# Transposes of the attention heads in two row tiles, the distance term summed on TensorE

## The chip, the cores and the metric

The kernel runs on one core of a Trainium2 chip. The metric is the device time of one execution in microseconds, the median of several runs. The core has five engines that run beside one another and wait for each other through semaphores: TensorE (PE, with its weight loads PEld), VectorE (DVE), ScalarE (ACT), GpSimd (POOL) and SyncE (SP), which issues DMAs. Each engine works through its instructions in the order in which the program gives them. SBUF is the working memory; TensorE writes into the eight banks of PSUM.

## The reference, cut to what matters

The program is a chain of four parts on a sequence of 2 x 1024 rows of 128 numbers: a Mamba block, a mixture of experts, six encoder layers (`L1_attn`), and a feed-forward part with 4-bit quantisation. The change is in the encoder. One of its layers is:

```python
rel = jnp.exp(-jnp.abs(pos[:, None] - pos[None, :]).astype(x.dtype) / DECAY)
...
scores = jnp.einsum('bhld,bmhd->bhlm', q, k) * inv_sqrt_d
w_avg = jax.nn.softmax(scores, axis=-1).mean(axis=1)
new_w = jax.nn.softmax(CSCALE * w_avg + rel[None], axis=-1)
sa = jnp.einsum('blm,bme->ble', new_w, h)
h1 = _ln(h + sa, l1w, l1b)
h2 = _ln(h1, l2w, l2b)
ff = jax.nn.relu(h2 @ w1.T + b1_) @ w2.T + b2_
return (_ln(h2 + ff, l3w, l3b), None)
```

There are H = 16 heads of 8 numbers, L = 1024 positions, 2 sequences and 6 layers, CSCALE = 1 and DECAY = 16. So each query has sixteen softmax rows of 1024, their mean, plus a term `rel` that depends on the distance alone, a second softmax, and a product with `h`.

## The kernel before

The encoder is the class `Encoder`. One attention is one layer of one sequence: 8 tiles of 128 queries (`m`), each with 16 heads (`hh`), 128 steps in all; 12 attentions make 1536 steps. `run` (L1067) writes the order of all engines out by hand, one step `s` after the other. A tile of 128 queries has its scores in 16 steps; the later stages of the same tile follow some steps behind. In each step:

- `scores` (L947): two matmuls of bf16 parts (72 x 128 weights, 72 x 512 moving, L963) put one head's scores of 128 queries into `sc`, a PSUM tile of two banks, of which there are three. VectorE takes the negated maximum `nm` of each row (L966).
- `exponentials` (L969): ScalarE writes `e = exp(sc + nm)` to SBUF and the row sums `z` with it (L972). The pool of `e` has 13 buffers.
- `scaled` (L981): every fourth step (GT = 4), VectorE takes the reciprocals of four heads' sums (L986), and GpSimd multiplies the four `e` by them (L989).
- `added` (L991), LAG = 10 steps behind: TensorE transposes the scaled `e` into `acc`, where the heads add up. A transpose is a matmul with a block of `e` (128 queries x 128 keys) as weights and the identity as the moving operand, and it accumulates in PSUM (L1008). `acc` is two tiles of one bank, each for 512 of the 1024 keys. In each of the four steps of a group of four heads, eight transposes are made: two heads in one half of the keys. Within a bank, the blocks of keys stand in reverse order.
- `shifted` (L1018), for each half of the keys: when its last head is in, VectorE forms `acc / 16 + rel` into the SBUF tile `mean` (L1022). `rel` is one array of 1920 columns, of which each tile takes a window.
- `second` (L1032): ScalarE takes the exponential of `mean` into `prT` (L1035). The two halves come two steps apart.
- `mixed` (L1043), four steps after the second of them: TensorE multiplies the transposed weights by `h`, with a column of ones for the sum (16 instructions at L1048, into `sa`, which is again one of the three score buffers). `residual` (L1057), one step later: VectorE divides and adds `h`.

Everything else of a layer (`between`, L885: norms, feed-forward with L904 and L918, transposes at L752; `project`, L810, for the next layer's queries and keys at L829, with their DMAs) is written as generators. `advance_one` (L1105) issues one piece of them in each step in which `mixed` doesn't stand, and two in each fourth.

TensorE's order in a step is therefore: scores, transposes, then a piece or the final product. The other engines see scores first, then the reductions, the scaling, the exponentials, then the second exponential.

Of the kernel before, what the change touches and what calls it, by code (L numbers as in the profile page):

```python
# [11 lines left out]
F32 = mybir.dt.float32  # L12
BF16 = mybir.dt.bfloat16
AF = mybir.ActivationFunctionType
ALU = mybir.AluOpType
# [3 lines left out]
P = 128  # L19
EPS = 1e-5  # L20
B, L, D = 2, 1024, 128
NT = B * L // P
TB = L // P
# [5 lines left out]
NL, NH, DH, FF = 6, 16, 8, 512  # L29
# [606 lines left out]
class Encoder:  # L636
# [10 lines left out]
    ROWS = 9 * DH  # L647
    GH = 4
    GT = 4
    LAG = 10  # L650
    TH = TB // 2
    HL = L // 2

    def __init__(self, c, ctx, x, w, t):
        self.c, self.nc, self.tc = c, c.nc, c.tc
        self.x, self.w, self.t = x, w, t
        nc, tc = self.nc, self.tc
        pool = lambda name, bufs, **kw: ctx.enter_context(tc.tile_pool(name=name, bufs=bufs, **kw))
# [12 lines left out]
        self.scale = float(DH) ** -0.5  # L671
        wp = self.wp

        nrel = 2 * L - P
        self.rel = wp.tile([P, nrel], F32, name="rel")
        nc.gpsimd.iota(
            self.rel,
            pattern=[[-1, nrel]],
            base=L - P,
            channel_multiplier=1,  # L680
            allow_small_or_imprecise_dtypes=True,
        )
        nc.scalar.activation(self.rel, self.rel, AF.Abs, bias=c.zero)
        nc.scalar.activation(self.rel, self.rel, AF.Exp, bias=c.zero, scale=-1.0 / DECAY)

        self.cols = {}
        for k in ("b1", "bq", "bk"):
            n = t[k].shape[0]
            src = t[k]
            if k != "b1":  # L690
                src = wp.tile([n, DH, NH], F32, name=f"e_{k}o")
                nc.gpsimd.tensor_copy(src, t[k].rearrange("l (h d) -> l d h", d=DH))
                src = src.rearrange("l d h -> l (d h)")
            ps = self.psum(f"ps_e_{k}")
            nc.tensor.transpose(ps[:, :n], src, c.ident[:n, :n])
            self.cols[k] = wp.tile([P, n], F32, name=f"e_{k}")
            nc.scalar.mul(self.cols[k], ps[:, :n], self.scale if k == "bq" else 1.0)
        self.eps = wp.tile([P, 1], F32, name="eps")
        nc.gpsimd.memset(self.eps, EPS)
        self.weights = {}  # L700
        self.h = [None] * B
        self.hn = [None] * B
        self.r = [None] * B
        self.qk = [None] * B
# [283 lines left out]
            e = a["e", s + i]  # L988
            nc.gpsimd.tensor_scalar(e, e, rz[:, i : i + 1], 1.0, ALU.mult, ALU.mult)  # L989

    def added(self, a, s, i):  # L991

        m, hh = divmod(s, NH)
        if hh == 0 and i == 0:
            a["acc", m] = [
                self.psa.tile([P, 4, P], F32, tag=f"acc{k}", name=f"acc_{a['who']}_{m}_{k}")
                for k in range(2)
            ]  # L1000
        half, two = divmod(i, 2)
        for j in (2 * two, 2 * two + 1):
            e = a["e", s + j]
            if half:
                del a["e", s + j]
            for n in range(4):
                at = (4 * half + n) * P
                self.nc.tensor.matmul(  # L1008
                    a["acc", m][half][:, 3 - n, :],
                    e[:, at : at + P],  # L1010
                    self.c.ident,
                    is_transpose=True,
                    start=hh + j == 0 and n == 0,
                    stop=hh + j == NH - 1,
                    skip_group_check=True,
                )

    def shifted(self, a, m, half):  # L1018

        t = self.loop.tile([P, self.HL], F32, tag="mean", name=f"mean_{a['who']}_{m}_{half}")  # L1020
        at = L - P - (4 * half + 3 - m) * P
        self.nc.vector.scalar_tensor_tensor(  # L1022
            t,
            a["acc", m][half].rearrange("p n q -> p (n q)"),
            1.0 / NH,
            self.rel[:, at : at + self.HL],
            ALU.mult,
            ALU.add,
        )
        a["mean", m, half] = t  # L1030

    def second(self, a, m, half):  # L1032

        t = self.loop.tile([P, 4, P], F32, tag="prT", bufs=4, name=f"prT_{a['who']}_{m}_{half}")
        self.nc.scalar.activation(  # L1035
            t.rearrange("p n q -> p (n q)"),
            a.pop(("mean", m, half)),
            AF.Exp,
            bias=self.c.zero,
        )  # L1040
        a["prT", m, half] = t

    def mixed(self, a, m):  # L1043

        prT = [a.pop(("prT", m, half)) for half in range(2)]
        sa = self.psum(f"sa_{a['who']}_{m}")
        for n in range(TB):
            self.nc.tensor.matmul(  # L1048
                sa[:, : D + 1],
                prT[n // 4][:, 3 - n % 4, :],  # L1050
                a["h"][:, n, :],
                start=n == 0,
                stop=n == TB - 1,
            )
        a["sa", m] = sa
# [11 lines left out]
    def run(self):  # L1067
        th = self.TH
        drain(self.layer(0))
        for b in range(B):  # L1070
            self.hn[b] = self.hidden(b, f"in_{b}")
            for half in range(2):
                hs = slice(half * th, half * th + th)
                src = self.x[:, b * TB : (b + 1) * TB, :][:, hs, :]
# [4 lines left out]
        n = NL * B * steps  # L1079
        lag, gt = self.LAG, self.GT  # L1080
        atts = {}
        work = []

        def add(b, pieces):
            work.append([b, pieces, None, 0])

        def advance(i, now):

            try:
                got = next(work[i][1])  # L1090
# [23 lines left out]
        def of(s):  # L1114
            return atts[s // steps], s % steps

        for half in range(2):
            add(1, self.project(0, 1, half))
        for s in range(n + lag + gt + 6):

            t = s - lag - gt - 5
            if t >= 0 and t % NH == NH - gt:
                a, ts = of(t)
                m = ts // NH
                if m % th == th - 1:
                    add(a["b"], self.between(a["l"], a["b"], m // th))
            if s < n:
                if s % steps == 0:
                    i = s // steps
                    while any(entry[0] == i % B for entry in work):  # L1130
                        advance(0, s)
                    atts[i] = self.begin(i)
                    if i % B == B - 1 and i // B + 1 < NL:
                        work.insert(0, [None, self.layer(i // B + 1), None, 0])
                self.scores(*of(s))
            release(s)
            t = s - lag - gt - 4
            if t >= 0 and t % NH == NH - gt:
                a, ts = of(t)
                self.residual(a, ts // NH)  # L1140
            if s % gt == 1 and gt < s <= n + 1:
                self.scaled(*of(s - gt - 1))
            t, i = divmod(s - lag, gt)
            t *= gt
            last = 0 <= t < n and t % NH == NH - gt and i % 2
            if 0 <= t < n:
                self.added(*of(t), i)
                if last:
                    a, ts = of(t)
                    self.shifted(a, ts // NH, i // 2)  # L1150
            if s < n:
                self.exponentials(*of(s))
            if last:
                self.second(a, ts // NH, i // 2)
            t = s - lag - gt - 3
            if t >= 0 and t % NH == NH - gt:
                a, ts = of(t)
                self.mixed(a, ts // NH)
            else:
                advance_one(s)  # L1160
        while work:
# [196 lines left out]
```

## Time and profile before

| What | Value |
|---|---|
| Median of 3 runs | 3520.73 us (3518.54 to 3523.78) |
| Profiled execution, its own time | 3524.13 us |
| Span in it | 3522.2 us |
| The twelve attentions | about 671 to 3296 us from the start |
| PE busy in 671 to 3296 | 2493.94 of 2625 us |
| PEld | 2001.04 us |
| DVE | 2090.61 us |
| ACT | 2139.69 us |
| POOL | 2149.08 us |
| Transposes of the heads, L1008 | 12288, mean 274 ns (PE), 141 ns (PEld) |
| Second exponentials, L1035 | 192, mean 713 ns |
| `acc / 16 + rel`, L1022 | 192, mean 672 ns |

The span is the time from the first to the last instruction of the program in the profiled execution; 1.9 us of that execution lie around it. In the profile, PE is a matmul and PEld the load of its weights; [...] matmuls that follow each other closely overlap in the records, and the distance of their starts says what one costs. A row of the busy slices has 40 digits, each the busy share of a slice in tenths. In a line of the timeline stand the start, the duration, the engine, the line of the kernel, the operation, what it writes and reads, the shapes and how many instructions are merged; in brackets stands how long the engine sat idle before, and what ended it.

### The profile page before, as it was taken

Reading aid. Unit: us, or ns where it says so; the run is one execution under the profiler, and the core shown is the slowest. Engines: PE = TensorE matmul, PEld = TensorE weight load, DVE = VectorE, ACT = ScalarE, POOL = GpSimd, SP = SyncE. Lnnn points to the kernel's source line nnn. Section 1 sums busy time; section 2 is a strip of 40 time slices with the busy share of each in tenths; the row PEclk is TensorE's granted clock in tenths of the full one; section 3 lists DMA queues with packets and bytes.
Section 4 is the critical chain, followed back from the end, with each engine's and each line's share of the span. In section 5 each row is a group of like instructions: output and inputs, shape, how many; then the busy total and the mean of one; then the engine's idle time right before and its main releaser. Section 6 shows DMA issues by size and latency. Waiting matters only on the chain. (4 is left out here: it accounts for less than half of the span.)

```text
span 3522.2 us, 56585 instructions
## 1 busy us (share of the span) xinstructions
PE 3054.7 (87%) x20551; PEld 2375.7 (67%) x20551; DVE 2632.6 (75%) x4250; ACT 2490.1 (71%) x4506; POOL 2519.8 (72%) x2791
## 2 busy tenths in 40 slices
PE   5655998488999999999999999999999999999635
PEld 2344665277777777777777777777777777778513
DVE  6888434277787887787877878778787787888487
ACT  4554343467887888888887888888888888888532
POOL 3998000577788887888878888788887888878622
PEclk8656999699999999999999999999999999999856
DMA  2454000410102112021120211202111021110000
GB/s 75 117 132 105 1 1 7 89 27 14 44 9 50 27 34 39 11 50 27 34 40 10 50 27 34 42 10 48 27 34 35 10 48 24 32 26 8 5 4 11
DMA packets 124043, 125.09 MB, mean 36 GB/s; under 512 B 13459, under 2 KB 102372, under 8 KB 120308
## 3 DMA queue, kind: packets, MB, share of 16 engines
q1 hardware_dynamic: 122900, 118.82, 16.4%
q8 instruction: 162, 2.65, 0.3%
q0 software_dynamic: 864, 2.66, 0.3%
q14 instruction: 117, 0.96, 0.1%
HBM read 101.25 MB, written 20.19 MB: 34 GB/s over the span
## 5 line engine op out<-in xcount | busy, mean ns | idle before, releaser
L966 DVE TENSOR_REDUCE nm<-sc 128x1 f32<-128x1024 f32 x1536 | 1851.0, 1219 | 565.2 <-PE sc L963 545.8
L972 ACT ACTIVATE e<-sc,nm 128x1024 f32<-128x1024 f32 x1536 | 1703.8, 1112 | 505.8 <-DVE nm L966 274.0
L989 POOL TENSOR_SCALAR e<-e,rz 128x1024 f32<-128x1024 f32 x1536 | 1689.3, 1120 | 384.6 <-DVE rz L986 367.7
L1008 PEld LDWEIGHTS acc<-ident,e 128*128 128x128 f32 x12288 | 1437.7, 141 | 369.6 <-POOL e L989 77.1
L1008 PE MATMUL acc<-ident,e 128*128 128x128 f32 x12288 | 1618.3, 274 | 35.2 <-POOL e L989 34.9
L963 PE MATMUL sc<-k,q 72*128 72x512 bf16 x3072 | 923.6, 382 | 116.7 <-ACT e L972 56.4
L963 PEld LDWEIGHTS <-q 72*128 72x128 bf16 x3072 | 302.2, 99 | 263.2 <-issue 227.5
L972 ACT ACTIVATION_READ_ACCUMULATOR e<-sc,nm 128x1 f32 x1536 | 298.1, 194 | 0.0
L286 PE MATMUL ys<-ident,yc 128*128 128x128 f32 x512 | 115.6, 390 | 103.1 <-POOL yc L418 85.6
L581 ACT ACTIVATE hT<-ph,b 128x512 f32<-128x512 f32 x128 | 87.9, 687 | 137.1 <-PE ph L574 134.8
L286 PEld LDWEIGHTS ys<-ident,yc 128*128 128x128 f32 x512 | 87.1, 201 | 138.3 <-POOL yc L418 103.2
L615 POOL TENSOR_TENSOR x<-fo,x 128x512 f32<-128x512 f32 x4 | 5.1, 1284 | 236.2 <-DVE fo L94 236.2
L598 DVE SCALAR_TENSOR_TENSOR eo<-po,hot,eo 128x128 f32<-128x128 f32 x256 | 72.0, 345 | 133.2 <-PE po L590 127.3
L369 POOL TENSOR_TENSOR db<-dtx,bb 128x512 f32<-128x512 f32 x128 | 161.2, 1292 | 0.2
L1048 PE MATMUL sa<-h,prT 128*128 128x129 f32 x1280 | 157.6, 275 | 1.2 <-ACT prT L1035 0.6
L1048 PEld LDWEIGHTS sa<-h,prT 128*128 128x128 f32 x1280 | 149.3, 191 | 4.1 <-ACT e L972 3.3
L590 PEld LDWEIGHTS po<-m_w,hT 128*128 128x128 f32 x1024 | 125.1, 195 | 30.5 <-ACT hT L581 15.7
L1035 ACT ACTIVATE prT<-mean,zero 128x512 f32<-128x512 f32 x192 | 137.0, 713 | 5.8 <-DVE mean L1022 5.8
L356 ACT ACTIVATE da<-dt,zero,na 128x512 f32<-128x512 f32 x128 | 99.8, 781 | 55.0 <-DVE hh L402 51.3
L1022 DVE SCALAR_TENSOR_TENSOR mean<-acc,rel 128x512 f32<-128x512 f32 x192 | 129.0, 672 | 6.8 <-PE acc L1008 6.8
L590 PE MATMUL po<-m_w,hT 128*128 128x128 f32 x1024 | 127.2, 278 | 0.0
L918 PE MATMUL ps_f<-w2T,ff 128*128 128x128 f32 x768 | 101.2, 275 | 0.1
(313 smaller groups left out, 2787.1 us busy)
## 6 DMA issues: line engine op xcount, KB each, us to landing
bb<-bcd SPq DMA_DIRECT2D x128, 256.0 KB
q<-d_bq SPq DMA_DIRECT2D x432, 64.0 KB
k<-d_bk SPq DMA_DIRECT2D x144, 192.0 KB
d_bq<-part_bq SPq DMA_DIRECT2D x72, 128.0 KB
d_bk<-part_bk SPq DMA_DIRECT2D x72, 128.0 KB
e_W<-in_L_attn_W SPq DMA_DIRECT2D x12, 256.0 KB
m_w<-in_L_ffn_W POOLq DMA_DIRECT2D x2, 1024.0 KB, 11.2
e_ln_w<-in_L_attn_ln_w SPq DMA_DIRECT2D x18, 64.0 KB
```

The lines of the kernel that those rows point to most:

```text
L286: nc.tensor.matmul(ys[k][:, t, :], src[:, t * P : (t + 1) * P], c.ident, is_transpose=True, start=first and t == 0, stop=last, skip_group_ ...
L369: nc.gpsimd.tensor_mul(db[g, k], dtx[b][:, k, halves[h]], bb[g][:, 0, :])
L590: nc.tensor.matmul(po[:, m, :], hT[:, k, m * P : (m + 1) * P], t["w2"][:, e, k, :], start=k == 0, stop=k == NHC - 1,)
L918: nc.tensor.matmul(ps[:, :P], ff[:, k, m * P : (m + 1) * P], tl["w2"][:, k * P : (k + 1) * P], start=k == 0, stop=k == NF - 1,)
L963: nc.tensor.matmul(sc[:, ss], q, qk["kt"][hh // self.GH][:, hh % self.GH, ss], start=True, stop=True)
L966: nc.vector.tensor_reduce(a["nm", m][:, hh : hh + 1], sc, AX.X, ALU.max, negate=True)
L972: self.nc.scalar.activation(e, a.pop(("sc", s)), AF.Exp, bias=a["nm", m][:, hh : hh + 1], accum_out=a["z", m][:, hh : hh + 1],)
L989: nc.gpsimd.tensor_scalar(e, e, rz[:, i : i + 1], 1.0, ALU.mult, ALU.mult)
L1008: self.nc.tensor.matmul(a["acc", m][half][:, 3 - n, :], e[:, at : at + P], self.c.ident, is_transpose=True, start=hh + j == 0 and n == 0, ...
L1022: self.nc.vector.scalar_tensor_tensor(t, a["acc", m][half].rearrange("p n q -> p (n q)"), 1.0 / NH, self.rel[:, at : at + self.HL], ALU.mu ...
L1035: self.nc.scalar.activation(t.rearrange("p n q -> p (n q)"), a.pop(("mean", m, half)), AF.Exp, bias=self.c.zero,)
L1048: self.nc.tensor.matmul(sa[:, : D + 1], prT[n // 4][:, 3 - n % 4, :], a["h"][:, n, :], start=n == 0, stop=n == TB - 1,)
```

## The change

The transposes of a head are split by halves of the queries. The first 64 queries are rows 0 to 63 of `e`, the other 64 rows 64 to 127. Each half is a matmul of its own, with 64 rows x 128 columns as weights and a 64 x 64 block of the identity as the moving operand. In the built program the first half has tile size 64 x 128 at position (0, 0) of the array, the second the same size at (64, 0); before, all transposes of heads were 128 x 128. The two `acc` banks now hold halves of the queries with all 1024 keys (8 x 64 numbers a partition) instead of halves of the keys.

`rel`, multiplied by 16 once at the start on GpSimd, is transposed into `acc` first, like a seventeenth head, and opens the accumulation. `shifted` goes; `second` reads `acc` itself with a scale of 1/16, in two instructions of 128 x 8 x 64, one for each bank, one after the other.

The lag falls from 10 to 8 steps. All blocks of one head are made in the same step. Counted from a tile's first step plus the lag, the steps 0 and 1 have no transposes, step 2 has `rel` and head 0, steps 7 and 12 have two heads, and each other step one. `second` stands in step 15, after the exponential of that step, `mixed` in step 17 (step 1 of the next tile), `residual` in step 18, and the pieces that follow a tile are added in step 19.

```diff
-    LAG = 10
+    LAG = 8
+
+    SUMS = [
+        (), (), (0,), (1,), (2,), (3,), (4,), (5, 6), (7,), (8,), (9,), (10,), (11, 12), (13,),
+        (14,), (15,),
+    ]
+    QS = (slice(0, P // 2), slice(P // 2, P))
...
         nc.scalar.activation(self.rel, self.rel, AF.Exp, bias=c.zero, scale=-1.0 / DECAY)
+        nc.gpsimd.tensor_scalar(self.rel, self.rel, float(NH), 0.0, ALU.mult, ALU.add)
...
-    def added(self, a, s, i):
...
-        half, two = divmod(i, 2)
-        for j in (2 * two, 2 * two + 1):
-            e = a["e", s + j]
...
-            for n in range(4):
-                at = (4 * half + n) * P
+    def onto(self, a, m, src, at, start, stop):
+        for n in range(TB):
+            for k, q in enumerate(self.QS):
                 self.nc.tensor.matmul(
-                    a["acc", m][half][:, 3 - n, :],
-                    e[:, at : at + P],
-                    self.c.ident,
+                    a["acc", m][k][:, TB - 1 - n, :],
+                    src[q, at(n) : at(n) + P],
+                    self.c.ident[q, q],
                     is_transpose=True,
-                    start=hh + j == 0 and n == 0,
-                    stop=hh + j == NH - 1,
+                    start=start and n == 0,
+                    stop=stop,
                     skip_group_check=True,
                 )
...
-    def shifted(self, a, m, half):
...
-        self.nc.vector.scalar_tensor_tensor(
-            t,
-            a["acc", m][half].rearrange("p n q -> p (n q)"),
-            1.0 / NH,
-            self.rel[:, at : at + self.HL],
-            ALU.mult,
-            ALU.add,
-        )
...
+    def offset(self, a, m):
+        a["acc", m] = [
+            self.psa.tile([P, TB, P // 2], F32, tag=f"acc{k}", name=f"acc_{a['who']}_{m}_{k}")
+            for k in range(2)
+        ]
+        self.onto(a, m, self.rel, lambda n: L - P - (m - n) * P, True, False)
+
+    def added(self, a, s):
+        m, hh = divmod(s, NH)
+        self.onto(a, m, a.pop(("e", s)), lambda n: n * P, False, hh == NH - 1)
+
+    def second(self, a, m):
+        t = self.loop.tile([P, TB, P], F32, tag="prT", name=f"prT_{a['who']}_{m}")
+        for k, q in enumerate(self.QS):
+            self.nc.scalar.activation(
+                t[:, :, q], a["acc", m][k], AF.Exp, bias=self.c.zero, scale=1.0 / NH
+            )
+        a["prT", m] = t
...
-                prT[n // 4][:, 3 - n % 4, :],
+                prT[:, TB - 1 - n, :],
...
+            if got := tile_at(s, NH + 2):
+                self.residual(*got)
             if s % gt == 1 and gt < s <= n + 1:
                 self.scaled(*of(s - gt - 1))
...
+            if 0 <= s - lag < n:
+                first = s - lag - (s - lag) % NH
+                for hh in self.SUMS[(s - lag) % NH]:
+                    a, t = of(first + hh)
+                    if hh == 0:
+                        self.offset(a, t // NH)
+                    self.added(a, t)
             if s < n:
                 self.exponentials(*of(s))
-            if last:
-                self.second(a, ts // NH, i // 2)
...
+            if got := tile_at(s, NH - 1):
+                self.second(*got)
+            if got := tile_at(s, NH + 1):
+                self.mixed(*got)
             else:
                 advance_one(s)
```

More of the change, by code (lines that the diff above doesn't have):

```diff
@@ L989, in scaled @@
             nc.gpsimd.tensor_scalar(e, e, rz[:, i : i + 1], 1.0, ALU.mult, ALU.mult)
-    def added(self, a, s, i):
[L995 to L1000, printed above, removed]
-        half, two = divmod(i, 2)
-        for j in (2 * two, 2 * two + 1):
-            e = a["e", s + j]
-            if half:
-                del a["e", s + j]
-            for n in range(4):
-                at = (4 * half + n) * P
+    def onto(self, a, m, src, at, start, stop):
+        for n in range(TB):
+            for k, q in enumerate(self.QS):
@@ L1015, in added @@
                     skip_group_check=True,
                 )
-    def shifted(self, a, m, half):
-        t = self.loop.tile([P, self.HL], F32, tag="mean", name=f"mean_{a['who']}_{m}_{half}")
-        at = L - P - (4 * half + 3 - m) * P
-        self.nc.vector.scalar_tensor_tensor(
-            t,
-            a["acc", m][half].rearrange("p n q -> p (n q)"),
-            1.0 / NH,
-            self.rel[:, at : at + self.HL],
-            ALU.mult,
-            ALU.add,
-        )
-        a["mean", m, half] = t
@@ L1032, in second @@
[L1032 to L1041, printed above, removed]
+    def offset(self, a, m):
[4 more added lines that the diff above has]
+        self.onto(a, m, self.rel, lambda n: L - P - (m - n) * P, True, False)
@@ L1043, in mixed @@
+    def added(self, a, s):
[8 more added lines that the diff above has]
+        a["prT", m] = t
     def mixed(self, a, m):
-        prT = [a.pop(("prT", m, half)) for half in range(2)]
+        prT = a.pop(("prT", m))
@@ L1118, in run, with tile_at @@
             add(1, self.project(0, 1, half))
-        for s in range(n + lag + gt + 6):
-            t = s - lag - gt - 5
-            if t >= 0 and t % NH == NH - gt:
+        def tile_at(s, o):
+            t = s - lag - o
+            if 0 <= t < n and t % NH == 0:
                 a, ts = of(t)
-                m = ts // NH
+                return a, ts // NH
+        for s in range(n + lag + 2 * NH):
+            if got := tile_at(s, NH + 3):
+                a, m = got
                 if m % th == th - 1:
@@ L1136, in run @@
             release(s)
[L1137 to L1140, printed above, removed]
+            if got := tile_at(s, NH + 2):
+                self.residual(*got)
             if s % gt == 1 and gt < s <= n + 1:
                 self.scaled(*of(s - gt - 1))
[L1143 to L1147, printed above, removed]
-                if last:
-                    a, ts = of(t)
-                    self.shifted(a, ts // NH, i // 2)
+            if 0 <= s - lag < n:
[5 more added lines that the diff above has]
+                    self.added(a, t)
             if s < n:
                 self.exponentials(*of(s))
-            if last:
-                self.second(a, ts // NH, i // 2)
[L1155 to L1158, printed above, removed]
+            if got := tile_at(s, NH - 1):
+                self.second(*got)
+            if got := tile_at(s, NH + 1):
+                self.mixed(*got)
             else:
```

## The prediction

> **What bounds the kernel now.** I read the page's busy row and slices, then the busy times of one attention (layer 3, batch 0: 128 steps, 1986.9 to 2206.0), then the timeline of single steps there, then the waits.
>
> ```profile
> PE   5655998488999999999999999999999999999635
> PEclk8656999699999999999999999999999999999856
> 1986.90:2206.00 219.10, 208.44 (x1513) 167.07 (x1513) 175.39 (x249) 179.20 (x324) 181.88 (x206) 1.00 0.17 33
> ```
>
> The last line gives the stretch's length, then PE, PEld, DVE, ACT and POOL busy, then the clock. PE is busy 208.4 of 219.1 us at full clock, no other engine above 182. The encoder (671 to 3296 us) holds twelve such attentions, 96 tiles of 16 heads.
>
> ```profile
> 2005.94 0.60 PE L963 MATMUL sc<-k,q 72*128 72x512 bf16 x2
> 2006.57 1.23 DVE L966 TENSOR_REDUCE nm<-sc 128x1 f32<-128x1024 f32 x1 [0.78 <-PE sc L963]
> 2007.24 0.60 PE L963 MATMUL sc<-k,q 72*128 72x512 bf16 x2
> 2007.47 1.01 PEld L1008 LDWEIGHTS acc<-ident,e 128*128 128x128 f32 x8
> 2007.68 1.04 PE L1008 MATMUL acc<-ident,e 128*128 128x128 f32 x8
> 2007.89 1.11 ACT L972 ACTIVATE e<-sc,nm 128x1024 f32<-128x1024 f32 x1 [1.00 <-DVE nm L966]
> 2008.55 0.60 PE L963 MATMUL sc<-k,q 72*128 72x512 bf16 x2
> 2009.00 0.71 ACT L1035 ACTIVATE prT<-mean,zero 128x512 f32<-128x512 f32 x1
> 2010.27 1.11 ACT L972 ACTIVATE e<-sc,nm 128x1024 f32<-128x1024 f32 x1 [0.57 <-DVE nm L966]
> 2011.53 0.59 PE L963 MATMUL sc<-k,q 72*128 72x512 bf16 x2 [0.19 <-ACT e L972]
> 2013.04 1.86 PEld L1048 LDWEIGHTS sa<-h,prT 128*128 128x128 f32 x16 [0.29 <-ACT e L972]
> 2014.83 0.21 PEld L963 LDWEIGHTS <-q 72*128 72x128 bf16 x2
> ```
>
> A plain step lasts 2008.55 - 2007.24 = 1.31 us and PE never pauses: 0.44 for two score matmuls (2007.24 to 2007.68), 0.87 for eight transposes of 109 ns. DVE and ACT idle 0.78 and 1.00 us before their part. With the final product (2013.04 to 2014.83, 1.79 us) a tile is 16 x 1.31 + 1.79 = 22.75 us of PE. Eight make 182 of the 219 us; the feed-forward, projection and other transposes are about 19 (start to start in the timeline: 64 x 0.112 at L918, 16 x 0.43 at L904, 8 x 0.43 at L829, 16 x 0.11 at L752), stalls and gaps the remaining 18.
>
> [...] The drain this trace does show, where a 128-column product changes to a 32-column mode and back:
>
> ```profile
> 122.54 0.27 PE L286 MATMUL ys<-ident,yc 128*128 128x128 f32 x1
> 122.74 0.14 PEld L247 LDWEIGHTS ps_x<-xc,xpT 128*32 128x32 f32 x2 [0.17 <-issue]
> ...
> 153.27 0.59 PE L247 MATMUL ps_x<-xc,xpT 128*32 128x512 f32 x1
> 153.79 0.14 PEld L286 LDWEIGHTS ys<-ident,yc 128*128 128x128 f32 x1 [0.84 <-DVE hh L402]
> ```
>
> The first product streams 0.109 us from 122.54; the next load starts 0.09 us after. The second streams 0.43 from 153.27; the load starts 0.09 after. Inside one mode the load starts with the product before it (2007.47, inside the scores of 2007.24). So a switch costs 0.09 us and uncovers the next load. [...]
>
> ```profile
> 3455.12 0.20 PEld L1289 LDWEIGHTS ps_hq<-ident,hq 128*128 128x128 f32 x2 [2.55 <-POOL hq L1215]
> 3455.18 0.24 PEld L1289 LDWEIGHTS ps_hq<-ident,hq 128*128 128x128 f32 x2
> ```
>
> Two loads on an idle array start about 0.057 us apart; I use that. [...]
>
> **The change part by part.**
>
> *Transposes.* Each of 8 becomes a pair, 64 rows by 128 columns as weights, 64 moving columns. [...] If both halves run side by side a pair costs 57, eight 0.456 instead of 0.87 us. Not shown in before: the bounds are 57 (all parallel) and 114 (loads one after the other). [...] 12288 pairs of load and product become 26112, rel's among them.
>
> *Mode switches.* Scores, final products and pieces use all rows, transposes 64. Each burst pays 0.09 + 0.057 on entry (first load uncovered) and 0.09 + 0.013 on exit (the page has bf16 loads at 99 ns against 141 for those of the transposes, so 0.042 under the 0.057), together 0.25 us. A step becomes 0.44 + 0.25 + 0.456 = 1.145 us.
>
> *Order.* The 16 heads are summed in 14 steps of a tile; head numbers 5/6 and 11/12 share a step, and rel goes before head 0. That is 14 switches in and 14 out, and three double steps of 1.60. From the step of rel to the step before the last: 10 x 1.145 + 3 x 1.60 = 16.25 us.
>
> *Rel and the second exp.* L1022 goes (192 x 0.67 us on DVE): PE hides DVE already, so nothing gained on the path. Rel costs PE 0.456 a tile, in the 1.60. The second exp stays 2 x 0.71 on ACT, from PSUM as L581 does (0.69); but both now stand in one place, behind the exponential of the last step, and the next tile's first transposes must wait for them, as must the final product. Rel times 16 is one GpSimd pass at the start, hidden.
>
> No DMA is added, and each stands where its scores stand; the pieces after a tile come four steps earlier (27 instead of 31 steps after its first scores).
>
> *The new wait.* Last burst: scores start at T, the burst ends at T + 1.145. Its exponential starts at T + 1.95 (2005.94 to 2007.89), the first second exp at T + 3.06 (2007.89 to 2009.00), the other ends about T + 4.4, and PE can load at T + 4.5. Meanwhile PE has two score steps without transposes, the second held to about T + 2.06 by a score buffer (an exponential frees its buffer 1.26 after its start: ACT at 2010.27, PE at 2011.53), done by T + 2.5. Then the final product stands at the head of PE's queue: 2 us of stall, with scores and so DVE and ACT queued behind it. It runs to T + 6.3, and the next scores start at T + 6.4. Tile: 16.25 + 6.4 = 22.65 against 22.75.
>
> *Sum.* -0.1 x 96 = -10 us. Pieces that fall in the stall are free: 19 us an attention over 16 positions, two of them there, 2.4, take 1.5: -18. GpSimd's scaling has less time: first needed 5, 5, 4, 3 steps after its issue instead of 5, and steps are shorter; PE waits for it 4.5 us an attention now, take 1 more: +12. The end of the encoder is four steps shorter: -3. On the profiled execution, 3524.13 (span 3522.2): 3524 - 10 - 18 + 12 - 3 = 3505; the median of the runs is 3.4 lower, so **3502 us**.
>
> **Rivals.**
>
> *A, slower: loads of the two halves do not overlap, so the change doesn't do what it says.* For: the 57 ns between loads is a load path busy for that long, and nothing here shows two in it. [...] Then 16 x 0.057 a head: step 1.60, double 2.51, tile 13 x 1.60 + 3 x 0.91 + 6.4 = 29.9, +7.15 x 96 = +690, less some 120 of present stalls that a slower PE covers: about 4090. It decides from a pair above about 58 ns on, because the tile's margin is 0.1 us over 136 pairs.
>
> *B, faster: the stall at the tile's end is largely filled* (pieces gather there, or a switch overlaps). Against: program order. Without half of its 2 us: -100, about 3400; all of it, 3300.
>
> *C, slower: PE no longer covers the others.* A plain step of 1.145 leaves DVE no room: two reductions back to back take 2.33 us in this trace, one 1.22, so they start 1.11 apart, and reciprocals and statistics come on top; the scaling's slack is cut. 6 to 8 us an attention: about 3590. For: with its reciprocals DVE needs about 1.15 a step. Against: the stall gives them time once a tile, and L1022 is gone.
>
> **How the numbers follow.** Forecast 0.46 (own range 3440 to 3570), A 0.17, B 0.18, C 0.19. Range 3340 to 3690: all but A and thin tails. A measurement here tells 0.2%, 7 us. Of the forecast's 0.46, 0.29 is faster, 0.06 the same, 0.11 slower. Faster 0.29 + 0.18 = 0.47, same 0.06, slower 0.11 + 0.19 + 0.17 = 0.47.
>
> **What would show it.** Pairs of transposes starting together, pairs 57 ns apart (57 for each half means A); 0.09 us before the first load of a burst and after it; plain steps of 1.15; a wait of PE for the second exp, about 2 us by 96; no DVE work at L1022. Wrong if the switch is free between these modes (then up to 340 us less), or the clock falls below 1.00 with half the array in use.

## The result and the profile after

| | before | after |
|---|---|---|
| Median | 3521.71 us (4 runs) | 3754.49 us (4 runs, 3752.37 to 3756.72) |
| Ratio | 1 | 1.0662, 95% interval 1.0643 to 1.0680 |
| Profiled execution, span | 3524.13, 3522.2 us | 3752.37, 3750.7 us |
| First to last scores of the encoder | 2624 us | 2858 us |
| of these at half TensorE clock | 57 us in 6 stretches | 643 us in 89 stretches |
| Mean of the 96 tiles | 27.33 us | 29.77 us |

The kernel is 6.6% slower where 0.5% less was forecast. All of it arose in the encoder: 2858 - 2624 = 234 us, or 2.44 us for each tile. (The half-clock figures here and below are summed from the clock record in the trace, between the first and the last scores. In the traces of before and after it holds two values, 1.00 and 0.50, in entries that last whole multiples of 3.413 us; one such length is called a window below. The figures belong to the one profiled execution of each kernel, whose time lies up to 16 us from the median.)

TensorE's busy row and its granted clock in the page of after, in 40 slices:

```profile
PE   5656994788998888988888888899888988889735
PEclk8657997777889988989888988898989898899756
```

Before, the clock row had a 9 in every full slice of the encoder. Now 7s and 8s stand all through it, so the loss is no matter of one place. The busy times of the attention of layer 3, batch 0, and of the whole encoder, in the kernel after (length, then PE, PEld, DVE, ACT and POOL busy, then the clock, DMA share and GB/s):

```profile
2106.30:2345.20 238.90, 211.72 (x2666) 137.91 (x2665) 165.31 (x232) 178.07 (x325) 182.36 (x206) 0.90 0.16 30
666.00:3526.00 2860.00, 2540.28 (x31802) 1628.20 (x31804) 1977.43 (x2749) 2133.74 (x3863) 2151.53 (x2398) 0.89 0.15 29
```

The attention took 219.1 us before. PE is busy 3 us longer (208.4 before), and idle 16 us longer: 27.2 against 10.7. Over the whole encoder PE is idle for 320 us, 189 more than before (131), and busy for 46 us more. No other engine came near its limit. But busy time is counted at the clock of the moment, as the groups of PE show, before and after (busy us and mean ns, then the idle time ahead of them and what ended it):

```profile
L1008 PE MATMUL acc<-ident,e 128*128 128x128 f32 x12288 | 1618.3, 274 | 35.2 <-POOL e L989 34.9
L1048 PE MATMUL sa<-h,prT 128*128 128x129 f32 x1280 | 157.6, 275 | 1.2 <-ACT prT L1035 0.6
```

```profile
L1005 PE MATMUL acc<-ident,e 64*128 64x64 f32 x24576 | 1103.0, 235 | 38.5 <-POOL e L996 38.0 <-POOL h L752 0.4
L1043 PE MATMUL sa<-h,prT 128*128 128x129 f32 x1280 | 264.3, 389 | 129.9 <-ACT prT L1033 112.2 <-ACT e L979 16.9 <-ACT hT_h L762 0.9
```

The transposes fell from 1618 to 1103 us, as intended. The final product wasn't touched, and its mean rose from 275 to 389 ns: half of the products run at half clock (50 of 96 start there; none did before). Part of one tile in the timeline of PE in after shows what a step does now (start, duration, then group; the idle time ahead in brackets):

```profile
2169.51 0.61 PE L970 MATMUL sc<-k,q 72*128 72x512 bf16 x2
2170.05 0.71 PE L1005 MATMUL acc<-ident,e 64*128 64x64 f32 x16
2170.69 0.61 PE L970 MATMUL sc<-k,q 72*128 72x512 bf16 x2
2171.23 0.71 PE L1005 MATMUL acc<-ident,e 64*128 64x64 f32 x16
2175.09 0.71 PE L1005 MATMUL acc<-ident,e 64*128 64x64 f32 x16 [3.16 <-POOL e L996]
2175.74 0.68 PE L970 MATMUL sc<-k,q 72*128 72x512 bf16 x2
2176.34 1.12 PE L1005 MATMUL acc<-ident,e 64*128 64x64 f32 x16
2177.39 1.04 PE L970 MATMUL sc<-k,q 72*128 72x512 bf16 x2
```

From 2169.51 to 2170.69 is a plain step, 1.18 us. At 2171.23 a step sums two heads; between the first and the second PE waits 3.16 us for GpSimd's scaling. The scores after it take 1.04 us for 0.61 (2177.39): the clock granted from 2177.39 to 2178.43 is 0.50. Now the end of a tile, PE and ACT together:

```profile
2119.92 0.61 PE L970 MATMUL sc<-k,q 72*128 72x512 bf16 x2
2120.46 0.71 PE L1005 MATMUL acc<-ident,e 64*128 64x64 f32 x16
2121.10 0.61 PE L970 MATMUL sc<-k,q 72*128 72x512 bf16 x2
2122.55 0.59 PE L970 MATMUL sc<-k,q 72*128 72x512 bf16 x2 [0.84 <-ACT e L979]
2122.82 1.11 ACT L979 ACTIVATE e<-sc,nm 128x1024 f32<-128x1024 f32 x1 [0.31 <-DVE mv_c L778]
2123.92 1.26 ACT L1033 ACTIVATE prT<-acc,zero 128x512 f32<-128x512 f32 x2
2125.23 3.54 PE L1043 MATMUL sa<-h,prT 128*128 128x129 f32 x16 [2.08 <-ACT prT L1033]
2128.61 0.60 PE L970 MATMUL sc<-k,q 72*128 72x512 bf16 x2
2129.14 0.71 PE L1005 MATMUL acc<-ident,rel 64*128 64x64 f32 x16
```

The last burst of transposes starts at 2120.46. Two bare score steps follow, then PE waits 2.08 us for the second exponentials (2123.92 to 2125.2). The product then takes 3.54 us, not 1.8, and the next scores start 8.7 us after those of the last burst (2128.61 - 2119.92). This tile is one of the longer ones: the mean over the tiles is 8.1 us. These waits, over the whole kernel, after and then before (total us, number of times, longest):

```profile
PE sa L1043 <- ACT prT L1033: 130.8, 78, 2.4
PE sc L970 <- ACT e L979: 95.4, 182, 2.9
PE acc L1005 <- POOL e L996: 38.0, 25, 3.2
```

```profile
PE sc L963 <- ACT e L972: 56.4, 167, 0.9
PE acc L1008 <- POOL e L989: 34.9, 67, 1.4
```

The first did not exist before (0.6 us at that product); the second was 56.4 us; the third 34.9 us in 67 short waits of 1.4 us at most, and is now 25 long ones.

### The profile page after: what moved, and what is told of

It reads as the page before. It is cut to its first block, busy times and chain, and to the rows that moved or that the text cites. A ratio compares the mean times of both kernels' runs of the same rounds, so it can differ in the third digit from the quotient of the medians.

```text
span 3750.7 us, 83946 instructions
## 1 busy us (share of the span) xinstructions
PE 3097.0 (83%) x34375; PEld 1998.2 (53%) x34375; DVE 2515.1 (67%) x4058; ACT 2485.3 (66%) x4506; POOL 2527.5 (67%) x2792
## 5 line engine op out<-in xcount | busy, mean ns | idle before, releaser
L1005 PEld LDWEIGHTS acc<-ident,e 64*128 64x128 f32 x24576 | 917.4, 145 | 606.3 <-issue 332.3
L1005 PE MATMUL acc<-ident,e 64*128 64x64 f32 x24576 | 1103.0, 235 | 38.5 <-POOL e L996 38.0
L970 PE MATMUL sc<-k,q 72*128 72x512 bf16 x3072 | 997.9, 410 | 147.3 <-ACT e L979 95.4
L970 PEld LDWEIGHTS <-q 72*128 72x128 bf16 x3072 | 233.9, 101 | 350.9 <-issue 244.7
L1043 PE MATMUL sa<-h,prT 128*128 128x129 f32 x1280 | 264.3, 389 | 129.9 <-ACT prT L1033 112.2
L1043 PEld LDWEIGHTS sa<-h,prT 128*128 128x128 f32 x1280 | 243.9, 293 | 173.6 <-ACT prT L1033 147.6
L1033 ACT ACTIVATE prT<-acc,zero 128x512 f32<-128x512 f32 x192 | 121.1, 687 | 5.4 <-PE acc L1005 5.4
L925 PE MATMUL ps_f<-w2T,ff 128*128 128x128 f32 x768 | 110.8, 287 | 1.8 <-ACT e L979 0.9
L911 PE MATMUL ps_f<-hT_h,w1T 128*128 128x512 f32 x192 | 109.1, 654 | 1.3 <-ACT hT_h L762 0.7
```

Of the source, the lines that this page charges most:

```text
L911: nc.tensor.matmul(ps[:, :hl], tl["w1"][:, k * P : (k + 1) * P], h2T, start=True, stop=True)
L925: nc.tensor.matmul(ps[:, :P], ff[:, k, m * P : (m + 1) * P], tl["w2"][:, k * P : (k + 1) * P], start=k == 0, stop=k == NF - 1,)
L970: nc.tensor.matmul(sc[:, ss], q, qk["kt"][hh // self.GH][:, hh % self.GH, ss], start=True, stop=True)
L1005: self.nc.tensor.matmul(a["acc", m][k][:, TB - 1 - n, :], src[q, at(n) : at(n) + P], self.c.ident[q, q], is_transpose=True, start=start an ...
L1033: self.nc.scalar.activation(t[:, :, q], a["acc", m][k], AF.Exp, bias=self.c.zero, scale=1.0 / NH)
L1043: self.nc.tensor.matmul(sa[:, : D + 1], prT[:, TB - 1 - n, :], a["h"][:, n, :], start=n == 0, stop=n == TB - 1,)
```

## The experiments

Three theories went in. **1**: the wait at the tile's end leaves TensorE so little to do that its clock is halved for the microseconds that follow. **2**: with LAG 8 the scaling comes too late for heads 11 and 12. **3**, the rival: working in row tiles, with a change of tiling mode in and out of each burst, is itself what costs. All times are medians; each ratio is to the kernel before on the same chip.

| Run | us | ratio (95%) | us at half clock (stretches) |
|---|---|---|---|
| after | 3754 | 1.0662 (1.0643 to 1.0680) | 643 (89) |
| e1, added matmuls | 3678 | 1.0455 (1.0432 to 1.0479) | 353 (31) |
| e2, second exp first | 3733 | 1.0598 (1.0567 to 1.0628) | 609 (74) |
| e3, LAG 10 | 3664 | 1.0402 (1.0385 to 1.0420) | 485 (77) |
| e4, full rows | 3701 | 1.0511 (1.0495 to 1.0527) | 155 (33) |
| e5, LAG 10 and added matmuls | 3612 | 1.0269 (1.0244 to 1.0293) | 215 (23) |
| e6, LAG 10 and pairs of heads | 3704 | 1.0520 (1.0493 to 1.0548) | 527 (76) |
| e7, rel on VectorE | 3774 | 1.0719 (1.0690 to 1.0748) | 678 (95) |
| v1, tile end rebuilt | 3598 | 1.0226 (1.0193 to 1.0258) | 424 (42) |
| v1 with full rows | 3596 | 1.0213 (1.0198 to 1.0228) | 49 (4) |
| r1, row tiles alone | 3643 | 1.0355 (1.0327 to 1.0383) | 513 (47) |
| v3, v1 and 4 added matmuls | 3577 | 1.0166 (1.0149 to 1.0183) | 229 (26) |
| v4, v1 and 6 added matmuls | 3549 | 1.0075 (1.0058 to 1.0093) | 223 (19) |
| v5n, v1 and late pieces | 3593 | 1.0222 (1.0184 to 1.0259) | 337 (40) |
| v5, v4 and late pieces | 3590 | 1.0193 (1.0176 to 1.0209) | 332 (19) |
| v7, v5 and 2 more matmuls | 3587 | 1.0183 (1.0155 to 1.0210) | 182 (17) |

**Is it the wait at the tile's end?** e1 gives TensorE something to do in it.

```diff
+        if s and hh == self.LAG:
+            self.idle(sc[:, :512], 4)
...
         sa = self.psum(f"sa_{a['who']}_{m}")
+        self.idle(sa[:, 512:], 6)
...
+    def idle(self, out, n):
+        for _ in range(n):
+            self.nc.tensor.matmul(out, self.warm[:, :P], self.warm, start=True, stop=True)
```

> Leaves nothing out; per tile 10 bf16 matmuls of 128x512 are added whose results are overwritten: 4 ahead of the scores of the step after the last burst (into their own bank) and 6 ahead of the product (into the bank beside it). About 2 us of TensorE work per tile, most of it inside the tile-end wait. Theory 1 (the tile-end wait, some 2 to 4 us with almost nothing on TensorE, has the clock halved for the 3.4 us that follow, so the product and the next steps run at half speed): the half-clock stretches of the encoder (643 us now) fall below 200 us, the product lasts about 1.8 us where it lasts 3.5 us, and the time falls from 3754 to 3500 to 3620 us. Theory 2 (GpSimd's scaling comes too late for heads 11 and 12 with a lag of 8): the 3.4 us waits for it stay, so not below 3580. Rival, theory 3 (the row tiles and their switches themselves cost the time, 14 switches of 0.25 us in a tile): the time stays at 3754 or rises by up to 190 us (96 tiles x 2 us of added work).

The time fell by 76 us although some 960 matmuls were added. PE's timeline at one tile's end in this kernel:

```profile
2100.20 0.72 PE L1010 MATMUL acc<-ident,e 64*128 64x64 f32 x16
2100.84 1.04 PE L1022 MATMUL sc<-warm 128*128 128x512 bf16 x4
2101.72 1.17 PE L975 MATMUL sc<-k,q 72*128 72x512 bf16 x4
2103.81 1.46 PE L1022 MATMUL sa<-warm 128*128 128x512 bf16 x6 [0.93 <-ACT e L984]
2105.10 1.95 PE L1053 MATMUL sa<-h,prT 128*128 128x129 f32 x16
2106.89 0.60 PE L975 MATMUL sc<-k,q 72*128 72x512 bf16 x2
```

The added matmuls stand at 2100.84 and 2103.81; the product behind them takes 1.79 us (2105.10 to 2106.89). Its instructions have a mean of 279 ns, and 6 of the 96 products start at half clock. Not all of theory 1's figures held: 353 us stay at half clock, more than the 200 expected, the time lies above the expected range, and the four matmuls ahead of the scores cost 0.9 us a tile (2100.84 to 2101.72), since PE doesn't wait there. The waits for GpSimd's scaling stay, 40.5 us, as theory 2 had it. Theory 3 alone, which had the time unchanged or longer, falls.

e2 shortens the wait by exchanging two instructions on ScalarE, the second exponentials and the exponential of the same step:

```diff
-            if s < n:
-                self.exponentials(*of(s))
             if got := tile_at(s, NH - 1):
                 self.second(*got)
+            if s < n:
+                self.exponentials(*of(s))
```

> The two second exponentials are issued ahead of the exponential of the same step, not after it. Theory 1: the wait for them is about 1.1 us shorter in each of 96 tiles (-105 us), and a shorter wait leaves fewer half-clock stretches, so 3580 to 3660 us and the half-clock time of the encoder clearly under 643 us. Theory 3 (row tiles and switches): the wait at the tile end isn't the price, at most -40 us. Against both: the exponential that is put back by 1.3 us holds the scores' bank, so that the wait moves to the next scores and the time stays.

Only -21 us, which misses theory 1's range and lies within what theory 3 allowed. The objection in the expectation explains it: the wait went from the second exponentials to the exponential that was put back and holds the product's buffer (121 us of waits of `sa` for `e`, where there were 20).

**Is it the scaling?** e3 is after with one number changed, `LAG = 10`.

> LAG 10 in place of 8, nothing else: two more steps between a head's exponential and its transposes. Theory 2: the two waits per attention of 3.4 us for GpSimd's scaled exponentials (heads 11 and 12) go, 12 x 2 x 3.4 = 80 us, and the time is 3660 to 3690 us. Theory 1 alone: the tile end is as before, 3745 to 3765 us; if those waits also drew half-clock stretches behind them, down to 3640. Theory 3: no change.

-90 us, within theory 2's range, but not made up as theory 2 had it. The groups of PE in this run:

```profile
L1005 PE MATMUL acc<-ident,e 64*128 64x64 f32 x24576 | 1070.7, 231 | 5.0 <-POOL e L996 4.9
L1043 PE MATMUL sa<-h,prT 128*128 128x129 f32 x1280 | 258.4, 383 | 113.7 <-ACT prT L1033 92.1 <-ACT e L979 18.2 <-ACT bk L841 3.4
```

The idle time for the scaling is 5 us where it was 38 us, so the waits themselves are 33 us and not 80; along with them 158 us at half clock went, and no other wait of PE changed by as much. The product still has 383 ns, so the tile's end is a separate loss.

**Is it the row tiles?** e4 undoes them alone: 128x128 transposes over the whole array, the sums split by keys.

```diff
-            for k, q in enumerate(self.QS):
-                self.nc.tensor.matmul(
-                    a["acc", m][k][:, TB - 1 - n, :],
-                    src[q, at(n) : at(n) + P],
-                    self.c.ident[q, q],
+            self.nc.tensor.matmul(
+                a["acc", m][n // 4][:, 3 - n % 4, :],
+                src[:, at(n) : at(n) + P],
+                self.c.ident,
```

> The row tiles alone are undone: each head is transposed in 8 blocks of 128x128 over the whole array, the sums split by keys over the two banks; rel's head, the lag and the two second exponentials as in the kernel after. Theory 1: the transposes cost 8 x 0.11 = 0.9 us a head where they cost 0.49 us and the switches of 0.25 us go, so a plain step is about 0.17 to 0.2 us longer and each tile 2 to 3 us: 3850 to 4000 us, unless TensorE is fuller and keeps its clock, which gives back up to 220 us: then 3700 to 3780. Theory 3 (the row tiles and their switches are what costs): below 3700 us, near the 3521 of the kernel before.

54 us faster than after, at the lower end of what theory 1 gave for a fuller TensorE, and just above the 3700 from which theory 3 was to begin. A plain step is back at 1.31 us; even so the kernel gains, because half-clock time is 155 us, not 643. The wait at the tile's end is still there (102 us for the second exponentials, where it was 131), yet 13 of the 96 products start at half clock and not 50. So the row tiles do cost something, through the clock; the layout of `acc`, and so how the second exponential reads it, changes with them.

e5 has LAG 10 and moves the added matmuls to where PE waits (3 ahead of the second bare scores, 6 ahead of the product).

> LAG 10, and 9 added bf16 matmuls of 128x512 a tile whose results are overwritten, now placed where TensorE waits: 3 ahead of the second bare score step, 6 ahead of the product; nothing left out. The run with LAG 10 alone took 3664 us with 485 us of the encoder at half clock. Theory 1 (the wait's low activity halves the clock in the next 3.4 us): half-clock time under 200 us, the step that holds the product falls from a mean of 5.1 us to about 3.8, time 3500 to 3570 us. If the clock follows the use of half the array instead, the half-clock time stays near 485 us and the time rises to 3664 to 3760.

-52 us against LAG 10 alone. Half-clock time fell from 485 to 215 us, near the 200 of theory 1; the time stayed 42 us above its range. Placed there, the three matmuls still cost 0.7 us a tile (the step before the product's rose from a mean of 1.52 to 2.24 us).

e6 has LAG 10 and the heads summed two at a time, with 8 bursts for 14:

```diff
-        (), (), (0,), (1,), (2,), (3,), (4,), (5, 6), (7,), (8,), (9,), (10,), (11, 12), (13,),
-        (14,), (15,),
+        (), (), (0, 1), (), (2, 3), (), (4, 5), (), (6, 7), (), (8, 9), (), (10, 11), (),
+        (12, 13), (14, 15),
```

> LAG 10, and two heads summed in every other step: 8 bursts a tile where there are 14, so 6 switches in and 6 out fewer, the same transposes. If switches of 0.25 us are on the path (theory 3, and the working of the forecast): 6 x 0.25 x 96 = 144 us under the 3664 of LAG 10 alone, 3500 to 3560. If ScalarE (1.31 us for each exponential with its readout, above a plain step's 1.18) takes over: at most -50, 3610 to 3660. Theory 1 adds half-clock stretches if the bare steps thin out the activity: then above 3664.

40 us slower than LAG 10 alone, with six mode changes in and six out fewer a tile. The waits of PE, largest first:

```profile
PE sc L970 <- ACT e L979: 208.5, 308, 3.6
```

With LAG 10 alone this was 90.2 us. Two scores back to back now run into buffers that ScalarE has not freed. So the saving expected from fewer switches did not show, and half-clock time rose from 485 to 527 us, as theory 1 allowed. What a switch costs by itself this run doesn't tell, since it brings waits of its own. (The expectation's 1.31 us an exponential was no bound: in the kernel after they start 1.09 us apart where nothing holds them, the readout of 0.19 us overlapping the exponentials before and after it by 0.11 us each.)

e7 undoes the other half of the change: rel is added by VectorE again.

```diff
-        self.onto(a, m, self.rel, lambda n: L - P - (m - n) * P, True, False)
...
+            self.nc.vector.scalar_tensor_tensor(
+                t, a["acc", m][k], 1.0 / NH, rel[:, :, q], ALU.mult, ALU.add
+            )
```

> The distance term alone is put back on VectorE: two scalar_tensor_tensor of 128x512, one for each query half, between the last burst and the second exponentials; no rel on TensorE, rel not scaled by 16. Row tiles, LAG 8 and order as in the kernel after. Theory 1: TensorE loses 0.49 us of work a tile (-47 us), but the two sums of 0.67 us lengthen the wait at the tile's end by 1.3 us (+125 us) and thin the activity: 3780 to 3950 us. If rel as another head is what costs (0.5 us and a switch-less burst that must wait for the second exponentials): below 3720.

19 us slower than after, just short of theory 1's range and far from the 3720 of the other: beside these row tiles and this order, rel as another head pays.

**The tile's end rebuilt.** v1 has LAG 10, the second exponentials first and split by keys, and the product one step earlier, in a buffer that is free:

```diff
+        for i in (1, 0):
...
+                t.rearrange("p n (k q) -> p k n q", k=2),
+                a["acc", m][:, :, i * TB // 2 : (i + 1) * TB // 2, :],
...
-            if got := tile_at(s, NH + 1):
+            if got := tile_at(s, NH):
                 self.mixed(*got)
```

> The tile end rebuilt, LAG 10: second exponentials ahead of the exponential of the same step and split by keys, not by queries, so that the product can begin after the first; the product one step earlier (right behind the next step's scores), so that its buffer is one that is already free; residual and pieces one step earlier. Nothing added or left out. Theory 1: the wait shrinks from about 2 to about 0.5 us, half-clock time under 150 us, the product 1.8 us; against LAG 10 alone -2 to -2.5 us a tile: 3420 to 3480 us. If ScalarE is the bound behind it (16 x 1.31 + 2 x 0.69 = 22.3 us a tile and its share of the pieces): 3480 to 3560. Theory 3 (row tiles and switches): no lower than 3600.

-66 us against LAG 10 alone, and above both of the faster ranges: it ends at the 3600 of theory 3, the rival. The product's wait for the second exponentials fell from 114 to 72 us and 19 products start at half clock, yet 424 us of it stay, and the stretches are longer: 424 / 42 = 10 us. So the tile was then tried with full rows, changed as in e4:

> The rebuilt tile end (3598 us, 424 us at half clock in 42 stretches, 10 us each) with the row tiles undone: 128x128 transposes over the whole array, the sums split by keys over the two banks; all else as there. If the clock is held down by the row tiles themselves (their work counts for less, so that it drops sooner and comes back later), the stretches get short, under 5 us each, and the half-clock time falls under 120 us, while plain steps rise from 1.18 to 1.31: 3540 to 3620. If only the waits set the clock, the half-clock time stays above 300 us and the time rises to 3680 to 3850.

The two kernels differ in nothing but the row tiles and the layout of `acc` that goes with them, and take the same time (3598 and 3596). The time and the 49 us at half clock are those expected if the row tiles themselves hold the clock down; the other branch, waits alone, had over 300 us. The four stretches that are left, 12 us each where under 5 were expected, all lie in the first attention. The same stretch of both, v1 first (length, PE, PEld, DVE, ACT and POOL busy, clock):

```profile
900.00:3300.00 2400.00, 2184.45 (x28493) 1390.30 (x28492) 1761.32 (x2480) 1913.03 (x3471) 1930.42 (x2177) 0.93 0.15 31
```

```profile
900.00:3300.00 2400.00, 2285.32 (x16991) 1875.79 (x16991) 1807.88 (x2502) 1939.30 (x3495) 1950.24 (x2195) 1.00 0.16 30
```

A clock of 0.93 against 1.00. In full rows PE is busy 101 us more in 2400, and gets as far; the row tiles' gain and their loss of clock cancel. With so little half clock this kernel is still 75 us above the kernel before. By an estimate rel accounts for that: in full rows a step of rel and one head has a median of 2.18 us, one with a head alone 1.31, and 0.87 us in 96 tiles are 83 us. Full rows with this tile's end and rel on VectorE were not tried.

r1 takes the opposite way: the kernel before, with its own order, and only its transposes in row tiles.

```diff
-                self.nc.tensor.matmul(
-                    a["acc", m][half][:, 3 - n, :],
-                    e[:, at : at + P],
-                    self.c.ident,
+                for k, q in enumerate(self.QS):
+                    self.nc.tensor.matmul(
+                        a["acc", m][:, k, TB - 1 - 4 * half - n, :],
+                        e[q, at : at + P],
+                        self.c.ident[q, q],
```

> The kernel before with the row tiles alone: its order (LAG 10, a quarter of four heads in each step, rel on VectorE, product three steps after the last quarter), but each 128x128 transpose as two of 64x64 in two row tiles, a bank for each query half; the first two quarters of a tile share its second step, and each half's sum on VectorE is two instructions of 128x4x64. Nothing left out. If the tile end is what costs (theory 1) and the row tiles work as forecast: plain steps fall from 1.31 to about 1.18 us, TensorE saves some 1 to 1.5 us a tile, the half-clock time of the encoder stays under 200 us: 3380 to 3480. If working in row tiles is what lowers the clock or ScalarE's 1.31 us for each exponential is the bound anyway: 3500 to 3600 and, in the first of these cases, over 300 us at half clock.

3.55% slower than before, above each expected range, with 513 us at half clock, for which the expectation had named the row tiles. Its waits:

```profile
PE sc L966 <- ACT e L975: 124.2, 293, 1.5
PE acc L1009 <- DVE mean L1024: 59.2, 88, 1.7
```

Before had 56.4 us in the first and none of the second: the next tile's first transposes wait for the sum on VectorE, since both halves of the keys now share the banks. So this run changed one wait besides the row tiles, and v1 with full rows is the cleaner comparison.

**What is left.** v3 and v4 add 4 matmuls to v1 ahead of the product, or 4 ahead of the first bare scores and 2 ahead of the product:

> The rebuilt tile end (3598 us, 424 us of the encoder at half clock) with 4 added bf16 matmuls of 128x512 ahead of the product, in the bank beside it, while it waits for the second exponentials (about 1.2 us); their results are not used. Theory 1: half-clock time under 150 us; each us at half clock costs about 0.4 us (a plain step 2.01 for 1.18), so 110 to 170 us less: 3430 to 3490. If the clock isn't set by activity at the tile end, it stays at 3598 or rises to 3640.

> The rebuilt tile end with the added matmuls placed ahead of the first bare scores (4) and ahead of the product (2), since the 4 ahead of the product waited themselves for their buffer (54 us) in the last such run (3577 us, 229 us at half clock). Theory 1: fewer windows of low activity at the tile end, under 150 us at half clock, 3520 to 3560. If the added 0.86 us ahead of the scores isn't hidden by the wait: 3580 to 3640.

v3 misses theory 1's range by 87 us, though it is 20 us faster than v1; v4 meets its range in time, though not in half-clock time. v4 is the best row-tiled kernel here, and still 0.75% above the kernel before. From 900 to 3300 us it has nine waits of 2.0 to 3.3 us ahead of scores, and eight are followed by 2 to 7 windows of half clock (6.8 to 24 us); the one at 2188 us comes from a piece, whose statistics on VectorE wait for GpSimd. Three runs let the pieces begin three steps later (`tile_at(s, NH + 5)` for `NH + 2`):

> The rebuilt tile end without added matmuls (3598 us), and the pieces after a tile begin three steps later (NH + 5 for NH + 2), so that their vector work meets GpSimd's scaling where it does in the kernel before. If the waits of 2.6 to 3.3 us of TensorE at these pieces, and the 4 to 7 half-clock windows behind each (seen in the run with added matmuls), are what is left: 25 to 60 us less, 3540 to 3575. If they only move: within 10 us of 3598.

> The rebuilt tile end with 4 added matmuls ahead of the first bare scores and 2 ahead of the product (3549 us, 223 us at half clock in 19 stretches), and the pieces three steps later. Six waits of 2 to 3.3 us go, and the stretches behind them: half-clock time under 130 us, 3490 to 3520, level with or below the kernel before at 3520. If they only move: 3540 to 3555.

> As the run with late pieces and added matmuls, and 2 more ahead of the second bare scores, where TensorE waits 0.4 us for an exponential. If activity at the tile end still starts half-clock stretches: 10 to 25 us below that run. If the 0.43 us aren't hidden: up to 20 us above it (96 x 0.2).

Nothing is gained. v5n is within the 10 us of v1 that were expected if the waits only move. v5 is 41 us slower than v4, above both of its ranges, with thirteen such waits of 1.9 to 2.7 us. v7 is level with v5, where 10 to 25 us less were expected; it has less half-clock time than v4 (182 for 223 us) and takes 38 us longer, so half-clock time alone doesn't order these runs: added matmuls are work too. No version tried beats the kernel before.

## Why the prediction was wrong

**Transposes: right.** The two halves overlap: their records start 3 ns apart, and pair follows pair after 62 ns (57 taken; that the halves run side by side was the author's assumption, which no trace of before showed). Rival A, no overlap, is out, although 62 ns lie above the 58 from which it was to decide: 5 ns over 136 pairs are 0.7 us a tile, more than the margin of 0.1 us that the forecast left.

**Mode switches: right.** A plain step at full clock is 1.18 us (1.145 forecast), a double one 1.67 (1.60). Of 1.18 us the scores take 0.44 and eight pairs 0.50, so 0.24 are left, which the working puts down to the switches in and out, though no run times one by itself (0.25 forecast; the working has 0.013 where 0.057 - 0.042 gives 0.015, which changes nothing). Over a tile's 13 steps before the last this is 0.04 x 10 + 0.07 x 3 = 0.6 us more, nearly all of it the 62 ns. That is 58 us in 96 tiles, enough to turn the forecast of -0.1 us a tile into a loss.

**The new wait: the step that failed.** It put the product's load at T + 4.5, its duration at 1.79 us, and the next scores at T + 6.4. Over the tiles the product starts at T + 5.0 in the mean, and the next scores at T + 8.1; in the tile shown above it is T + 5.3, 3.5 us and T + 8.7. The early part was somewhat short: the exponential starts at T + 2.35 in the mean, not T + 1.95, and in the tile shown at T + 2.9, because VectorE had statistics of a piece between its reductions. The larger error is the product, 3.0 us to the next scores for 1.9: the forecast priced the stall as idle time at a constant clock. PE's idle time as a whole came out about as forecast: 189 us more over the encoder, where a stall of 2 us a tile makes 192. What failed is the saving in busy time that was to pay for it. PE is busy 46 us longer, because work at half clock takes longer (the product 3.5 us for 1.79). That the wait halves the clock behind it is shown by e1, which fills it and gets the product back to full speed (a mean of 279 ns for 389, 6 of 96 starting at half clock for 50), with no other change. In the kernel after it does so together with the row tiles: in full rows nearly the same wait leaves 155 us at half clock (e4). The steps that follow suffer too: the step of rel and head 0 has a median of 2.24 us for 1.60, and 57 of 96 start at half clock.

**The clock had no term in the sum.** The forecast listed, under what would make it wrong, a clock below 1.00 with half the array in use, and gave it neither price nor chance. It came about: full rows take the half-clock time from 643 to 155 us (e4) and from 424 to 49 us (v1). In the kernel after, full rows would have been 54 us faster (e4). The loss can't be divided between waits and row tiles: filling the waits (e1) and undoing the row tiles (e4) each take a large part of the half-clock time away.

**Scaling waits: right mechanism, wrong size.** +12 us was forecast; LAG 10 takes away 90 (e3). Only 33 of them are idle time; steps behind a wait of 3.2 us also ran at half speed. This is rival C's second half. Its price of 88 us over the forecast is near the 90, but by luck, since it had no clock in it. Its first half, VectorE without room, has at most the 0.4 us a tile by which the exponential at the tile's end starts late.

**Pieces hidden in the stall, -18 us: not shown.** No run isolates it; v4 shows a piece making a wait of its own.

**Rel on TensorE: right, small.** Nothing gained on the path was forecast, with 0.456 us in a double step; e7 puts it 19 us ahead of VectorE's sum.

**The sum.** Forecast -0.1 us a tile, measured +2.44. Taken off in turn: scaling 90 us, the tile's end rebuilt 66 us, added matmuls 49 us (v4), which leave 28 of the 233 us. That the row tiles still lose in v4 through the clock is likely, with 223 us at half clock, but what would remove it was not found.

## What to carry to other kernels

Before shortening TensorE's work next to a wait, ask what share of the next few microseconds it will still be busy. Here the wait cost its own length (2.08 us in the tile shown), and behind it 50 of 96 products started at half clock (3.54 us for 1.79 in that tile). A chain that only one step feeds (last transpose, exponential, product) needs other TensorE work beside it (76 us less in e1), and a shorter lag needs its leads counted anew, each head by itself (90 us less with LAG 10). A transposing burst that is faster by itself can be worth nothing when the clock is lower with it: v1 had a clock of 0.93 in row tiles and 1.00 in full rows (900 to 3300 us), and took 3598 and 3596 us. So compare the clock of the stretch, not only the busy time.

## What the runs showed of the hardware

**The clock changed in steps of 3.413 us.** In the traces of before and after, the clock record has 190 entries between the first and the last scores of the encoder. Each holds 1.00 or 0.50 and lasts a multiple of 3.413 us, within 2 ns. In after, 47 of the 89 stretches at half clock last one window, and the longest lasts ten (34 us). They followed windows with little work, and windows that were mostly busy could be enough: in after, of the windows at full clock in which PE was busy below 40%, all 39 were followed by half clock; between 40 and 75%, 49 of 76; above, none of 534. What decided it between 40 and 75% was not shown.

**In row tiles the same busy share went with half clock more often.** Of full-clock windows with PE busy 60 to 70%, none of 64 was followed by half clock in e4, with full rows; in row tiles it was 20 of 27 (after), 13 of 31 (v1), 20 of 29 (r1). And of the half-clock windows with PE busy 95% or more, 1 of 27 was followed by another in e4, but 49 of 125 in after, 65 of 103 in v1, and 82 of 129 in r1. The busy share is taken from the records of the products, whose ends are modelled, and no run shows why row tiles differ.

**Transposes went with a full clock.** The encoder of v1 with full rows is mostly transposes (1565 us of PE), and its clock is 1.00 from 900 to 3300 us. Its other work alone would not explain that: in 249 of its windows at full clock TensorE's other work covered 30 to 40%, and none was followed by half clock, while every window with less than 40% of all work was (4 of 4 in e4, 39 of 39 in after).
